# A graph network stack on one core: attention scores transposed once for four edge chunks, softmax results in four transposes, blocks 32 partitions apart

## The chip, the cores and the metric

The kernel runs on one core of a Trainium2 chip. The core's engines run side by side, each with its own queue of instructions in fixed order: TensorE (PE, matmuls and transposes through the array, with its weight loads listed as PEld), VectorE (DVE), ScalarE (ACT), GpSimd (POOL) and SyncE (SP, which issues DMAs). The metric is the device time of one execution in microseconds. Four timed runs of the kernel before took 3209.85 to 3216.49 us, with a median of 3212.87.

## The reference

The input is x, 128 graphs of 128 nodes with 256 features, and one 128 x 128 adjacency matrix. Four layers follow each other, each as layer_norm(x + layer(x)): a graph attention with four heads over 512 edges, a three-step convolution, a layer with three weight matrices and a bias, and a layer with two batch norms. The change touches only the first one, the attention:

```python
Xq = (H @ W_lin.T).reshape(bt, n, h, dh)
Xv = (H @ W_val.T).reshape(bt, n, h, dh)
e = jnp.einsum('behd,hd->beh', leaky_relu(Xq[:, src] + Xq[:, dst], 0.2), a)
e = e + jnp.log(A0[src, dst] + EPS)[None, :, None]
m = segment_max(e over edges with the same src)
ex = jnp.exp(e - m[src])
attn = ex / segment_sum(ex)[src]
Y = segment_sum(attn * Xv[:, dst])
return Y @ W_out.T
```

For each graph and head there is thus a score per edge, and a softmax over the edges that leave the same node.

## The kernel before

The 128 graphs are taken in 32 quads of 4 graphs. A quad has 4 graphs x 4 heads = 16 rows (R) of scores, and 512 edges (E), which lie sorted by their source node in 4 chunks (NE) of 128 edges.

The main loop, `iteration(k)` (lines 789 to 889), is a software pipeline: in one pass, quad k - 1 finishes its third layer and starts the fourth, quad k goes through the second layer's middle product (`second`, lines 520 to 606) and its last (`third`), quad k + 1 has its attention summed and starts the second layer, quad k + 2 (called e) has scores and softmax, and quad k + 3 (g) has its queries computed and its gathers issued. Passes k = 1 to 29 have a quad e. Quads 0, 1 and 2 have their scores and softmax in `start` and `iteration_0`. The order of the instructions on each engine is that of the code: the whole part stands under a manual schedule.

The steps of quad e that the change touches, in their order:

- `gather` and `gather_last` (POOL queue) bring the query rows of source and destination of each edge into a tile z of 128 edges x 1024; `score(k, c)` (lines 338 to 349) makes the leaky relu, the product with a and the sum over 64 features on DVE (L344, L346, L347). The 16 scores of 128 edges go to `es[:, c, :]`, edges on partitions. After the last chunk, L349 adds the logarithm of the weights.
- `softmax_parts(k)` (lines 351 to 371) is a generator whose pieces `iteration` calls between matmuls. Its first piece transposes the four chunks on PE (L356), each 128 x 16 to 16 x 128, side by side into one PSUM bank `pe`, so that 16 rows lie on partitions and 512 edges run along the row. The segment maximum is two running scans on DVE, forward (L358) and backward (L361), with a mask that resets them where the source node changes. L364 subtracts on DVE, L365 takes the exponent on ACT, and two more scans (L367, L369) make the segment sum.
- `attention(k)` (lines 373 to 383) turns exponent f and sum m back on PE in eight transposes of 16 x 128 to 128 x 16 (L379), takes the reciprocal (L381) and multiplies (L383) on DVE. `scatter` then writes the result to DRAM by four indirect DMAs from POOL's queue, and SP loads it as a dense matrix for the next pass.

In `iteration`, the first piece of the softmax is called after `stage_f` (L697, the fourth layer's first product of quad k - 1), and the others between the products of `queries` and `hidden` (L280 and L726), whose block sums are L180 to L190 on DVE. In `second`, `after(i)` calls what the list `between[i]` holds after the i-th product: scores of chunks 1 to 3 after products 0, 2 and 7, copies of attention rows after 1, 3, 8 and 10, and the transposes of the inputs of quad g (L237) after 11. After product 12 there is nothing in the list. `attention(e)` follows the first half of `third` (L616) and stands before `mix1` (L441).

PSUM has 8 banks, all handed out from one pool (`ps`).

Of the kernel before, what the change touches and what calls it, by code (L numbers as in the profile page):

```python
# [8 lines left out]
F32 = mybir.dt.float32  # L9
# [3 lines left out]
ALU = mybir.AluOpType  # L13
# [6 lines left out]
EPS = 1e-5  # L20
BIG = 1e38
DROP = -1e30


@with_exitstack
def gnn_stack(ctx: ExitStack, tc: tile.TileContext, x, adj, w_qv_t, a, w_out_t, src, dst,
# [14 lines left out]
    nc = tc.nc  # L41
    B, N, D = x.shape
    H, DH = a.shape
    E = src.shape[0]
    P = 128
    assert N == P and D == 2 * P and E == 4 * P and H * DH == D and DH == 64
    NE = E // P
# [3 lines left out]
    R = QB * H  # L51
# [9 lines left out]
    def ctile(shape, name, dtype=F32, pool=const):  # L61
        return pool.tile(shape, dtype, tag=name, name=name)

    def ps(name):
        return psum.tile([P, 512], F32, tag="ps", name=name)
# [6 lines left out]
    ident = ctile([P, P], "ident")  # L72
# [55 lines left out]
    with ExitStack() as phase:  # L128
        cst = phase.enter_context(tc.tile_pool(name="cst", bufs=1))
# [69 lines left out]
        ws = phase.enter_context(tc.tile_pool(name="ws", bufs=2))  # L199
        wk = phase.enter_context(tc.tile_pool(name="wk", bufs=2))  # L200
# [19 lines left out]
        keep_b = ctile([R, E], "keep_b", BF16, cst)  # L220
        reset_f = ctile([R, E], "reset_f", BF16, cst)
        reset_b = ctile([R, E], "reset_b", BF16, cst)


        def temp(name):
            return wk.tile([P, 512], F32, tag="t", name=name, bufs=6)

# [110 lines left out]
        def score(k, c):  # L338

            s = quads[k]  # L340
            if c == 0:
                s.es = ws.tile([P, NE, R], F32, tag="es", name=f"es{k}", bufs=1)
            z = s.z[c]
            nc.vector.scalar_tensor_tensor(z, z, SLOPE, z, op0=ALU.mult, op1=ALU.max)  # L344
            z3 = z.rearrange("p (b d) -> p b d", d=D)
            nc.vector.tensor_mul(z3, z3, a_bc.unsqueeze(1).to_broadcast([P, QB, D]))  # L346
            nc.vector.reduce_sum(s.es[:, c, :], z.rearrange("p (r d) -> p r d", d=DH), axis=AX.X)  # L347
            if c == NE - 1:
                nc.vector.tensor_add(s.es, s.es, log_col.unsqueeze(2).to_broadcast([P, NE, R]))  # L349

        def softmax_parts(k):

            s = quads[k]
            pe = ps("pe")
            for c in range(NE):
                nc.tensor.transpose(pe[:R, c * P:(c + 1) * P], s.es[:, c, :], ident)  # L356
            f = wk.tile([R, E], F32, tag="f", name="f", bufs=1)
            nc.vector.tensor_tensor_scan(f, reset_f, pe[:R, :], initial=0.0, op0=ALU.add, op1=ALU.max)  # L358
            yield
            m = wk.tile([R, E], F32, tag="m", name="m", bufs=1)  # L360
            nc.vector.tensor_tensor_scan(m[:, ::-1], reset_b[:, ::-1], f[:, ::-1], initial=0.0,  # L361
                                         op0=ALU.add, op1=ALU.max)
            yield
            nc.vector.tensor_sub(f, pe[:R, :], m)  # L364
            nc.scalar.activation(f, f, AF.Exp)  # L365
            yield
            nc.vector.tensor_tensor_scan(m, keep_f, f, initial=0.0, op0=ALU.mult, op1=ALU.add)  # L367
            yield
            nc.vector.tensor_tensor_scan(m[:, ::-1], keep_b[:, ::-1], m[:, ::-1], initial=0.0,  # L369
                                         op0=ALU.mult, op1=ALU.max)  # L370
            s.ex, s.den = f, m

        def attention(k):

            s = quads[k]
            pa = ps("pat")[:, :2 * NE * R].rearrange("p (s c r) -> p s c r", s=2, c=NE)
            for i, t in ((0, s.ex), (1, s.den)):
                for c in range(NE):
                    nc.tensor.transpose(pa[:, i, c, :], t[:, c * P:(c + 1) * P], ident[:R, :R])  # L379
            rden = wk.tile([P, NE, R], F32, tag="rden", name="rden", bufs=1)  # L380
            nc.vector.reciprocal(rden, pa[:, 1])  # L381
            s.at = wk.tile([P, NE, R], F32, tag="at", name="at", bufs=1)
            nc.vector.tensor_mul(s.at, rden, pa[:, 0])  # L383

        def scatter(k):
            s = quads[k]
# [64 lines left out]
        def first(k, i):  # L451
            s = quads[k]
            ph = ps("ph")
            for dc in range(DC):
                nc.tensor.matmul(ph, s.mx[i // 2 * 2][:, i % 2, dc, :], w1_sb[:, dc, :],
                                 start=(dc == 0), stop=(dc == DC - 1))
            h1 = temp("h1")
            nc.scalar.activation(h1, ph, AF.Relu)
            for c in range(K1):
                s.h1[i, c] = h1[:, c * P:(c + 1) * P]  # L460
# [328 lines left out]
        def iteration(k):  # L789
            a, c, b, e, g = k - 1, k, k + 1, k + 2, k + 3  # L790
            has_c, has_b, has_e, has_g = c < NQ, b < NQ, e < NQ, g < NQ
            if has_b and b > 2:
                quads[b].xr = load_x(b)
            if has_c:
                late_sums(c)
            parts = quads[a].layer2 if a > 0 else iter(())
            for _ in range(3):
                next(parts, None)
            if has_e:
                score(e, 0)  # L800
                gather_last(e)
            for _ in parts:
                pass
            if has_c:
                between = {i: [] for i in range(14)}
                if has_e:
                    for c_, i in enumerate((0, 2, 7)):
                        between[i].append(lambda c_=c_: score(e, c_ + 1))
                if has_b:
                    for j, i in enumerate((1, 3, 8, 10)):  # L810
                        between[i].append(lambda j=j: by_row(b, j))
                if has_g:
                    between[11].append(lambda: values_in(g, quads[g].xg))
                second(c, between)
            if has_g and g + 1 < NQ:
                quads[g + 1].xg = load_x(g + 1, "xg", 1, ws)
            if has_c:
                room = room_of("m2", 7)
            if has_g:
                q = queries(g, room[:5])  # L820
            stage_f(a)
            if not has_c:
                for i in range(K3):
                    hidden_last(a, i)
                return
            steps = softmax_parts(e) if has_e else iter(())
            next(steps, None)
            h = hidden(a, room[5:] + room[2:4])
            if has_g:
                run(q.p1, q.p5, q.p2)  # L830
                next(steps, None)
                q.p6()
            run(h.p1, h.p5)
            next(steps, None)
            if has_g:
                q.p7()
            run(h.p2, h.p6)
            next(steps, None)
            if has_g:
                run(q.p4, q.p3)  # L840
                spill(g)
            next(steps, None)
            h.p7()
            if has_b:
                aggregate(b)
            run(h.p4, h.p3)
            hidden_stats(a)
            if has_g:
                gather(g)
            if has_b:  # L850
                stage_a(b)
            next(steps, None)
            for _ in third(c, 0):
                pass
            if has_e:
                attention(e)
                scatter(e)
            rest = third(c, 2)
            if not has_b:
                next(rest)  # L860
                third_mix(c, 0)
                third_norm(c, 0)
                for _ in rest:
                    pass
                third_mix(c, 2)
                third_norm(c, 2)
                quads[c].layer2 = stage_e(c)
                next(quads[c].layer2)
                return
            mix1(b, 0)  # L870
            mix1(b, 2)
            third_mix(c, 0)
            next(rest)
            w = first_seven(b)
            third_norm(c, 0)
            next(rest)
            run(w.p1, w.p5, w.p2)
            next(rest)
            w.p6()
            next(rest, None)  # L880
            w.p7()
            third_mix(c, 2)
            w.p4()
            w.p3()
            third_norm(c, 2)
            quads[c].layer2 = stage_e(c)
            next(quads[c].layer2)
            for i in range(QB):
                mix2(b, i)

        def iteration_0():
# [14 lines left out]
            for _ in third(0, 0):  # L906
                pass
            steps = softmax_parts(2)
            next(steps)
            for j in (0, 1):  # L910
                by_row(1, j)
# [31 lines left out]
        def start():  # L943
# [106 lines left out]
                    nc.vector.tensor_copy(att_idx, pc[:, :, 0])  # L1050
                    nc.vector.tensor_copy(log_col, pc[:, :, 1])
            steps = softmax_parts(0)
            for _ in range(2):
                next(steps)
            values_in(2, quads[2].xr, nc.scalar.copy)
            next(steps)
# [65 lines left out]
            mix1(0, 2)  # L1122
            steps = softmax_parts(1)
            first(0, 0)
            next(steps)
            second_sums()
            for i in range(QB):
# [311 lines left out]
```

## Time and profile before

| | |
|---|---|
| median of four timed runs | 3212.87 us |
| the profiled execution, its own time | 3209.69 us |
| its span in the profile | 3208.0 us |
| PE busy, share of the span | 97% |
| DVE, ACT and POOL busy | 67%, 40% and 21% |
| score transposes on PE (L356) | 128, 273 ns each from start to modelled end |
| softmax transposes on PE (L379) | 256, 208 ns each |
| scans on DVE (L358, L361, L367, L369) | 32 of each, 1.20 to 1.21 us |
| reciprocal on DVE (L381) | 32, 556 to 558 ns |

A line of the profile in order of time has the start and the duration in microseconds, the engine, the line of the code, the operation with what it writes and reads, the shapes, and a count of merged instructions. For PE, 128*16 128x128 means a weight tile of 128 partitions x 16 columns and 128 x 128 moved values. Matmuls overlap in the array, so the distance between two starts says more than a duration. A bracket at the end of a line is the time that the engine was idle before, and what ended it.

### The profile page before, as it was taken

How to read it: one execution, taken by the hardware profiler on the slowest of the kernel's cores; microseconds unless marked ns; L12 is line 12 of the kernel's file. 1: busy time of each engine (PE TensorE's matmuls, PEld its weight loads, DVE VectorE, ACT ScalarE, POOL GpSimd, SP SyncE). 2: the span in 40 equal slices, each digit the busy share in tenths (PEclk: the TensorE clock that was granted, in tenths of full speed). 3: DMA queues.
4: the chain of work that ended last, by engine and by line, in shares of the span. 5: the costliest groups of instructions: out<-in, count | busy, mean ns of one | idle time of the engine just before them, and what ended most of it. 6: DMA issues, size and time to landing. Idle time of an engine off the chain costs nothing. (4 is left out here: it accounts for less than half of the span.)

```text
span 3208.0 us, 41204 instructions
## 1 busy us (share of the span) xinstructions
PE 3125.3 (97%) x15884; PEld 2589.4 (81%) x15884; DVE 2144.3 (67%) x4200; ACT 1277.8 (40%) x2229; POOL 662.7 (21%) x541
## 2 busy tenths in 40 slices
PE   6999999999999999999999999999999999999997
PEld 3788888888888888888888888888888888874444
DVE  6666666666666666666666666666666666437888
ACT  2343333333333343333333333343333333326668
POOL 4211222112111111222112111111222111001135
PEclk7999999999999999999999999999999999999999
DMA  7613333333333223333333333223333331005557
GB/s 217 182 50 96 106 99 106 98 94 106 101 91 104 88 77 96 106 99 106 99 93 106 100 92 104 87 76 97 106 99 106 99 87 53 21 27 184 177 194 272
DMA packets 118756, 344.86 MB, mean 108 GB/s; under 512 B 15008, under 2 KB 51744, under 8 KB 110240
## 3 DMA queue, kind: packets, MB, share of 16 engines
q0 software_dynamic: 45552, 151.55, 19.4%
q1 hardware_dynamic: 70960, 188.71, 16.3%
q8 instruction: 126, 2.06, 0.3%
q10 hardware_dynamic: 2048, 1.97, 0.2%
q14 instruction: 70, 0.57, 0.1%
HBM read 256.20 MB, written 85.98 MB: 107 GB/s over the span
## 5 line engine op out<-in xcount | busy, mean ns | idle before, releaser
L535 PE MATMUL ph<-m,w 128*128 128x256 f32 x2048 | 464.0, 380 | 0.0
L616 PE MATMUL p<-w,h 128*128 128x256 f32 x2048 | 462.3, 379 | 0.0
L616 PEld LDWEIGHTS p<-w,h 128*128 128x128 f32 x2048 | 389.0, 190 | 66.1 <-issue 7.7
L535 PEld LDWEIGHTS ph<-m,w 128*128 128x128 f32 x2048 | 387.4, 190 | 51.5
L329 POOL DMA_INDIRECT zs<-qd,src_idx x123 | 119.8, 974 | 1390.4 <-DVE z L739 706.0
L535 PE MATMUL ph<-m,w_s 128*128 128x256 f32 x1536 | 352.4, 379 | 0.0
L666 PE MATMUL po<-l2w,ms 128*128 128x256 f32 x1536 | 347.7, 379 | 1.3 <-DVE ms L658 1.3
L535 PEld LDWEIGHTS ph<-m,w_s 128*128 128x128 f32 x1536 | 291.8, 190 | 39.7
L666 PEld LDWEIGHTS po<-l2w,ms 128*128 128x128 f32 x1536 | 284.4, 190 | 36.2 <-DVE ms L658 1.5
L329 POOL DMA_INDIRECT zs<-qd,dst_idx x123 | 210.5, 1712 | 254.5 <-DMA zs<-qd,src_idx 243.3
L112 ACT ACTIVATE ln_sd<-ln_mv,eps 128x2 f32<-128x2 f32 x192 | 56.3, 293 | 496.7 <-DVE ln_mv L107 496.7
L548 DVE TENSOR_TENSOR h<-ph,u 128x512 f32<-128x512 f32 x128 | 88.1, 689 | 167.7 <-PE ph L535 114.5
L389 POOL DMA_INDIRECT attd<-at,att_idx x128 | 126.1, 985 | 351.3 <-DMA attd<-at,att_idx 248.0
L542 ACT COPY u<-ph 128x512 f32<-128x512 f32 x128 | 75.0, 586 | 244.2 <-PE ph L535 244.2
L346 DVE TENSOR_TENSOR zs<-zs,a_bc 128x1024 f32<-128x1024 f32 x123 | 150.8, 1226 | 4.2
L347 DVE TENSOR_REDUCE es<-zs 128x16 f32<-128x1024 f32 x123 | 150.1, 1220 | 4.2
L344 DVE SCALAR_TENSOR_TENSOR zs<-zs 128x1024 f32<-128x1024 f32 x123 | 149.6, 1217 | 2.1 <-DMA zs<-qd,dst_idx 2.1
L654 ACT COPY ms<-pm 128x512 f32<-128x512 f32 x128 | 71.2, 580 | 194.4 <-PE pm L652 191.0
L105 DVE BATCH_NORM_STATS2 ln_st<-xr 128x6 f32<-128x256 f32 x384 | 144.2, 417 | 5.5
L120 DVE TENSOR_SCALAR xr<-xr,ln_mv,ln_rs 128x256 f32<-128x256 f32 x384 | 143.1, 414 | 7.0
L477 DVE TENSOR_TENSOR h<-z,adc 128x512 f32<-128x512 f32 x62 | 41.9, 675 | 153.9 <-ACT adc L471 153.9
L640 POOL TENSOR_TENSOR xb<-xr,bias 128x512 f32<-128x512 f32 x64 | 81.6, 1275 | 298.3 <-DVE xr L120 160.3
(298 smaller groups left out, 5702.4 us busy)
## 6 DMA issues: line engine op xcount, KB each, us to landing
ad<-attd SPq DMA_DIRECT2D x32, 1024.0 KB, 4.8
zd<-z SPq DMA_DIRECT2D x31, 1024.0 KB, 7.4
zl<-zd SPq DMA_DIRECT2D x62, 512.0 KB, 3.5
xr<-in_x_dram SPq DMA_DIRECT2D x32, 512.0 KB, 5.8
x3d<-xr SPq DMA_DIRECT2D x32, 512.0 KB, 2.8
x3l<-x3d SPq DMA_DIRECT2D x32, 512.0 KB, 5.2
out_dram<-x3l POOLq DMA_DIRECT2D x31, 512.0 KB, 5.1
qd<-qt SPq DMA_DIRECT2D x30, 512.0 KB, 2.6
```

The lines of the kernel that those rows point to most:

```text
L105: nc.vector.bn_stats(st[:, i, :], r[:, i, :])
L120: nc.vector.tensor_scalar(r[:, i, :], r[:, i, :], mv[:, i, 0:1], rs[:, i:i + 1], op0=ALU.subtract, op1=ALU.mult)
L329: nc.gpsimd.indirect_dma_start(out=s.z[c], out_offset=None, in_=s.qd, in_offset=bass.IndirectOffsetOnAxis(ap=idx[:, c:c + 1], axis=0), com ...
L344: nc.vector.scalar_tensor_tensor(z, z, SLOPE, z, op0=ALU.mult, op1=ALU.max)
L346: nc.vector.tensor_mul(z3, z3, a_bc.unsqueeze(1).to_broadcast([P, QB, D]))
L347: nc.vector.reduce_sum(s.es[:, c, :], z.rearrange("p (r d) -> p r d", d=DH), axis=AX.X)
L389: nc.gpsimd.indirect_dma_start(out=ad, out_offset=bass.IndirectOffsetOnAxis(ap=att_idx[:, c:c + 1], axis=0), in_=s.at[:, c, :], in_offset= ...
L535: nc.tensor.matmul(bank[g][:, i].rearrange("p b n -> p (b n)"), wa[:, c, f:f + P], s.m2[:, blk_b, c].rearrange("p b n -> p (b n)"), start= ...
L548: nc.vector.tensor_add(block(g, row, col), bank[g], kept_[g])
L616: nc.tensor.matmul(p3[:, t * D:(t + 1) * D], s.h2[f // 2][:, f % 2, j + t, :], w3_sb[:, f, :], start=(f == 0), stop=(f == K2 - 1))
L640: nc.gpsimd.tensor_add(s.xb[:, j:j + 2, :], xj, bias.unsqueeze(1).to_broadcast([P, 2, D]))
L666: nc.tensor.matmul(po[:, i % 2, :], mss[i][:, t, dc, :], l2w[:, t, dc, :], start=(n3 == 0), stop=(n3 == 3 * DC - 1))
```

## The change

Two tiles are made once and cleared: `scores`, 128 edges x 4 chunks x 32 places, of which the first 16 hold scores, and `pair`, 48 partitions x 512 edges. A constant GAP = 32 is the distance of blocks.

The scores of all four chunks are transposed as one 128 x 128 matrix: chunk c comes out on partitions 32 c to 32 c + 15. Four copies on ACT put the four blocks side by side into partitions 0 to 15 of `pair` (f). The scans and the subtract read f in SBUF where they read PSUM before. The last scan writes the sum to partitions 32 to 47 of `pair`. So exponent and sum of a chunk lie in one tile of 48 partitions, and `attention` turns them back with one transpose a chunk: columns 0 to 15 are the exponent, 32 to 47 the sum.

The generator has one piece more, since transpose and copies are now apart from the first scan. In `iteration` that new first piece is called in `second` after product 12, and the piece with the first scan stays after `stage_f`, as do all later ones. In `start` and `iteration_0` there is one more call at the old place of the first.

```diff
+        scores = ctile([P, NE, GAP], "scores", pool=cst)
+        pair = ctile([GAP + R, E], "pair", pool=cst)
+        nc.vector.memset(scores, 0.0)
+        nc.vector.memset(pair, 0.0)
...
-                s.es = ws.tile([P, NE, R], F32, tag="es", name=f"es{k}", bufs=1)
+                s.es = scores[:, :, :R]
...
-            pe = ps("pe")
+            f, m = pair[:R], wk.tile([R, E], F32, tag="m", name="m", bufs=1)
+            rows = f
+            pe = ps("pe")[:, :P]
+            nc.tensor.transpose(pe, scores.rearrange("p c r -> p (c r)"), ident)
             for c in range(NE):
-                nc.tensor.transpose(pe[:R, c * P:(c + 1) * P], s.es[:, c, :], ident)
-            f = wk.tile([R, E], F32, tag="f", name="f", bufs=1)
-            nc.vector.tensor_tensor_scan(f, reset_f, pe[:R, :], initial=0.0, op0=ALU.add, op1=ALU.max)
+                nc.scalar.copy(f[:, c * P:(c + 1) * P], pe[c * GAP:c * GAP + R, :])
             yield
-            m = wk.tile([R, E], F32, tag="m", name="m", bufs=1)
-            nc.vector.tensor_tensor_scan(m[:, ::-1], reset_b[:, ::-1], f[:, ::-1], initial=0.0,
+            nc.vector.tensor_tensor_scan(m, reset_f, rows, initial=0.0, op0=ALU.add, op1=ALU.max)
+            yield
+            nc.vector.tensor_tensor_scan(m[:, ::-1], reset_b[:, ::-1], m[:, ::-1], initial=0.0,
                                          op0=ALU.add, op1=ALU.max)
             yield
-            nc.vector.tensor_sub(f, pe[:R, :], m)
+            nc.vector.tensor_sub(f, rows, m)
...
-            nc.vector.tensor_tensor_scan(m[:, ::-1], keep_b[:, ::-1], m[:, ::-1], initial=0.0,
+            nc.vector.tensor_tensor_scan(pair[GAP:, ::-1], keep_b[:, ::-1], m[:, ::-1], initial=0.0,
                                          op0=ALU.mult, op1=ALU.max)
-            s.ex, s.den = f, m
...
-            pa = ps("pat")[:, :2 * NE * R].rearrange("p (s c r) -> p s c r", s=2, c=NE)
-            for i, t in ((0, s.ex), (1, s.den)):
-                for c in range(NE):
-                    nc.tensor.transpose(pa[:, i, c, :], t[:, c * P:(c + 1) * P], ident[:R, :R])
+            pa = ps("pat")[:, :NE * (GAP + R)].rearrange("p (c r) -> p c r", c=NE)
+            for c in range(NE):
+                nc.tensor.transpose(pa[:, c, :], pair[:, c * P:(c + 1) * P], ident[:GAP + R, :GAP + R])
...
-            nc.vector.reciprocal(rden, pa[:, 1])
+            nc.vector.reciprocal(rden, pa[:, :, GAP:])
...
-            nc.vector.tensor_mul(s.at, rden, pa[:, 0])
+            nc.vector.tensor_mul(s.at, rden, pa[:, :, :R])
...
+            steps = softmax_parts(e) if has_e else iter(())
             if has_c:
                 between = {i: [] for i in range(14)}
+                between[12].append(lambda: next(steps, None))
...
-            steps = softmax_parts(e) if has_e else iter(())
             next(steps, None)
```

More of the change, by code (lines that the diff above doesn't have):

```diff
@@ L22 @@
 DROP = -1e30
+GAP = 32
 @with_exitstack
@@ L908, in iteration_0 @@
             steps = softmax_parts(2)
+            next(steps)
             next(steps)
@@ L1052, in start @@
             steps = softmax_parts(0)
-            for _ in range(2):
+            for _ in range(3):
                 next(steps)
@@ L1124, in start @@
             first(0, 0)
+            next(steps)
             next(steps)
```

## The prediction

> **What bounds the kernel now.** I read the page's busy table first, then a table by stage for one pass of the main loop, then the instructions in order of time: TensorE (PE) alone, and ScalarE (ACT) and VectorE (DVE) around the places that the change touches. The chain that ended last holds only the last microsecond, so it does not help.
>
> The busy table, and one pass (here 1425.50 to 1512.70 us: total, then busy time of PE, PE weight load, DVE, ACT and POOL, granted clock, DMA share, GB/s):
>
> ```profile
> PE 3125.3 (97%) x15884; PEld 2589.4 (81%) x15884; DVE 2144.3 (67%) x4200; ACT 1277.8 (40%) x2229; POOL 662.7 (21%) x541
> ...
> 1425.50:1512.70 87.20, 87.20 (x469) 76.10 (x468) 58.40 (x113) 32.92 (x56) 17.02 (x14) 1.00 0.34 98
> ```
>
> PE is busy for all 87.20 us of the pass, at full clock; DVE and ACT have 28.8 and 54.3 us to spare. So in a steady pass only PE time counts, as long as no wait is made. Next, PE in order of time (start, duration, engine, line, tiles, count):
>
> ```profile
> 1443.50 1.04 PE L237 MATMUL pt<-ident,xg 128*128 128x128 f32 x8
> 1444.37 1.89 PE L535 MATMUL ph<-m,w 128*128 128x256 f32 x8
> 1446.10 1.89 PE L535 MATMUL ph<-m,w_s 128*128 128x256 f32 x8
> 1447.83 1.95 PE L697 MATMUL pa<-ahat_t,xr 128*128 128x128 f32 x16
> 1449.61 0.60 PE L356 MATMUL pe<-ident,es 128*16 128x128 f32 x4
> 1450.05 1.03 PE L280 MATMUL y<-wqv,xt 128*128 128x256 f32 x4
> ...
> 1474.68 0.41 PE L379 MATMUL pat<-ident,f 16*128 16x16 f32 x4
> 1474.95 0.39 PE L379 MATMUL pat<-ident,m 16*128 16x16 f32 x4
> 1475.28 2.05 PE L441 MATMUL pm<-wt_t,xr 128*128 128x128 f32 x16
> ```
>
> Matmuls overlap, so I price by the distance from start to start. The four score transposes hold PE for 1450.05 - 1449.61 = 0.44 us (0.11 each). Eight whole 128x128 transposes (L237) take 1444.37 - 1443.50 = 0.87, also 0.109 each: a transpose's price here follows its 128 moved columns, not the 16 or 128 weight columns. The eight softmax transposes take 1475.28 - 1474.68 = 0.60: 0.27 for the first four (0.0675 each), 0.33 for the last four with the change back to full matmuls. Last, the covers on DVE and ACT (a bracket is idle time and what ended it):
>
> ```profile
> 1441.78 0.23 DVE L349 TENSOR_TENSOR es<-es,log_col 128x64 f32<-128x64 f32 x1
> 1446.79 0.62 ACT L552 ACTIVATE h<-h 128x512 f32<-128x512 f32 x1
> 1448.75 0.63 ACT L552 ACTIVATE h<-h 128x512 f32<-128x512 f32 x1 [1.34 <-DVE h L548]
> 1449.42 1.31 ACT L700 COPY ag<-pa 128x512 f32<-128x512 f32 x2
> 1450.25 1.21 DVE L358 TENSOR_TENSOR_SCAN f<-reset_f,pe 16x512 f32<-16x512 bf16 x1
> ```
>
> **The change part by part.** Passes k = 1 to 29 have a softmax: 29 steady ones. Quads 0, 1 and 2 have theirs in the start.
>
> *Scores.* Four transposes become one of the same form as L237: 0.44 - 0.11 = 0.33 saved on PE, 29 x 0.33 = 9.6 us. Bounds 0.27 (one semaphore event, 0.05 in the rows of L356, lands on PE) to 0.35.
>
> The Trainium skill, "TensorE: Matmul & The Clock Gate", section "LDWEIGHTS (loading the stationary operand)", speaks against this: it prices a weight load at columns / 1.2 ns, so 128 columns cost an estimated 107 ns where 16 cost 13, and if that stood in the open the saving would fall by 29 x 0.09 = 2.7 us; L237's 0.109 with the same load says it is hidden.
>
> *Place.* The transpose moves from behind L697 to before the last product of the second layer: start 1446.10 instead of 1449.61. It waits for L349, which ends at 1442.01: 4.1 us of slack (at k = 1, where L349 starts at 219.30 and that product at 221.29, 1.8). Behind it in PE's queue stand that product, L697 and everything after. They come 0.11 later until L697 ends and 0.33 earlier from L280 on. No DMA issue moves on any queue, POOL's and SP's order is the old one.
>
> *Four ACT copies* replace nothing. Bounds: the 128x256 copy (L503) takes 0.37, the 128x512 one 0.59 (L542), so 0.84 ns per column and about 0.27 for 128 columns; back to back, two 512-column copies of L654 take 1.05, 0.11 less than twice 0.58. So four take 0.27 + 3 x 0.16 = 0.75 at best and 4 x 0.37 = 1.49 at worst; I take 0.85, between single and overlapped copies of their own size. They stand between the two relus above, where ACT is idle for 1.34 us: nothing. At 1.49 they push the second relu and the L700 copies by 0.15; those end at 1450.73 and PE first reads them at 1453.50. Cover gone by 2.6 us more would be needed before PE noticed. The first scan, at 1450.25, waits for these copies (about 1448.3) instead of PE: nothing.
>
> *DVE.* Scans and subtract stay in their places with the same sizes (1.20 and 0.68); reading f from SBUF instead of PSUM is bounded by L358's 1.208 against L361's 1.203. DVE runs on 0.11 late while PE runs 0.33 early, so DVE loses 0.44 of lead: the block sum of L188 ends at 1452.11 and PE wants it at 1454.37; the exponent's input is ready at 1455.46 and ACT, with its table load, asks at 1456.46. Both leads outlive 0.44. The two clears go to DVE before its first input lands (it idles 5.4 us until 7.06): nothing.
>
> *PSUM.* One bank is asked for earlier and given back after the copies instead of after the subtract (1455.46). In the built order L697's second bank now follows a relu that ended at 1442.57; PE wants it at about 1448. No wait.
>
> *Softmax transposes.* Eight become four, with 48 rows and 48 moved columns instead of 16. Each is at least the 0.0675 of today and at most the 0.109 of a full one. 0.0675 at 16 columns and 0.109 at 128 are the nearest rows; I take 0.095, because the weight load is seen not to be pulled ahead here (0.33 us idle on PEld before L379), and then the 32 extra columns come on top at the 0.85 ns of L237 (0.027). So 4 x 0.095 + 0.06 for the change back = 0.44, which saves 0.16; 29 x 0.16 = 4.6 us. With the bounds 0.10 to 0.27: 2.9 to 7.8.
>
> The Trainium skill, "TensorEngine Tiling (Array Packing)", section "Key Properties", says that a change of tiling mode drains TensorE. At L379 the trace shows it (0.09 us before, and it stays, since 48 rows are a part of the array too); at L356 it shows none: L697's sixteen take 1.78 = 16 x 0.111 into it. By the rule the score part would save another drain at each end, an estimated 29 x 0.18 = 5 us; by the rows nothing, and I take the rows.
>
> *Once.* The start is not PE-bound:
>
> ```profile
> 97.50 0.60 PE L356 MATMUL pe<-ident,es 128*16 128x128 f32 x4
> 97.76 0.60 ACT L458 ACTIVATE h<-ph 128x512 f32<-128x512 f32 x1 [1.24 <-PE ph L455]
> 98.14 1.21 DVE L358 TENSOR_TENSOR_SCAN f<-reset_f,pe 16x512 f32<-16x512 bf16 x1 [2.78 <-PE pe L356]
> 106.93 0.63 ACT L365 ACTIVATE f<-f 16x512 f32<-16x512 f32 x1 [2.56 <-DVE f L364]
> 108.08 2.08 PE L498 MATMUL pm<-wt_t,h 128*128 128x128 f32 x8 [2.15 <-ACT h L458]
> ...
> 2675.91 1.10 PE L726 MATMUL z<-ag,l3w_s 128*128 128x256 f32 x4 [1.06 <-DVE ag L188]
> ```
>
> Quad 1: the copies queue behind L458 (to 98.3), so the scan starts near 99.25; DVE has no gap until the subtract, the exponent is 1.1 late, the relu behind it too, and PE at 108.08: +1.1. Quad 0: copies 0.85 - 0.5 from the faster transposes (slower clock there), about +0.3 on a chain to the attention load. Quad 2: -0.3. At k = 29 the scan no longer waits for PE in front of the block sums, and the 1.06 wait of the last row goes: -1.0. Together +0.1, bounds -1.5 to +1.5.
>
> **Sum.** -9.6 - 4.6 + 0.1 = -14.1 against the profiled execution's own 3209.69 us (span 3208.0): 3195.6. That execution lies 3.2 below the median of the four timed runs, 3212.87; on the median's scale 3198.8. I forecast 3199.
>
> **Rivals.**
> - *Only the scores pay.* If four 48-row transposes take what eight took (0.135 each, the duration of today's 16*128 weight load), 29 x 0.33 = 9.6 is left: 3203. For it: that load is not overlapped with the matmul before it. Against: two of today's, load and all, fit in 0.135.
> - *Hidden anyway.* If something beside PE set the pass at 87.2, nothing moves: 3210 to 3213. Against: no PE wait in a steady pass, 54 us of idle ACT, a third of the DMA.
> - *Slower: PE waits for the scores at the new place.* One mechanism: the last chunk's gather lands late, L349 follows, and PE, in order, stands still before the last product. At k = 1 DVE does wait 2.15 us for that gather and the slack is down to 1.8. It decides when the scores come 4.6 us later than in the pass shown (4.1 of slack and the 0.49 won); each further microsecond costs 29. A wait of 1 us a pass makes 3199 + 29 = 3228. Against: DVE's scores run without a DMA wait in the pass shown, and all that feeds them moves with PE.
> - *The change isn't made.* Excluded: the built program has 1 and 4 transposes a quad, and four copies.
>
> **How the numbers follow.** As forecast 0.72; only scores 0.13; hidden 0.06; slower by a new wait 0.09. About 0.2% (6.4 us) is what a measurement of this kernel can tell from no change. Likeliest case alone: gains of 29 x 0.37 - 1.5 = 9.2 to 29 x 0.62 + 1.5 = 19.5, that is 3193 to 3204, and 1 us for the scatter of the medians: 3192 to 3205. The range over all, 3191 to 3206, takes in the second case. Faster 0.84 (both gaining cases less a little), same 0.07, slower 0.09.
>
> **What would show it.** Right: a steady pass of 86.6 to 86.8 us, still all PE; one pe transpose holding PE 0.11; four pat transposes from 0.33 to 0.50 to the next matmul; ACT's four copies between the relus; no wait of PE on L349's successor. Wrong: PE idle before the pe transpose or before the hidden products, copies over 0.4 us each, or pat transposes over 0.13 each.

## The result and the profile after

The changed kernel takes 3217.25 us (median of 32 runs, 3215.42 to 3218.97), the kernel before 3213.49 (52 runs, 3208.55 to 3216.91). The ratio is 1.0015, with a 95% interval of 1.001 to 1.002: slower by 0.15%, within the 0.2% that was called no change. The forecast was 3199, range 3191 to 3206. The profiled execution of the changed kernel has a span of 3215.4 us, the one of before 3208.0.

First the busy table of the kernel after:

```profile
PE 3119.5 (97%) x15660; PEld 2574.0 (80%) x15660; DVE 2147.9 (67%) x4202; ACT 1302.3 (41%) x2357; POOL 663.5 (21%) x541
```

PE has 224 instructions fewer, ACT 128 more. The change is made as described, and yet PE is not done earlier. A steady pass runs from the first fourth-layer product (called pa here, after the tile that it writes) to the same product one pass later. Before, it took 87.47 us, from 1447.83, shown in the prediction, to 1535.29 (with unrounded starts). PE in order of time, before:

```profile
1456.95 1.03 PE L726 MATMUL y<-ag,l3w_s 128*128 128x256 f32 x4
1457.82 1.03 PE L280 MATMUL y<-wqv_s,xt 128*128 128x256 f32 x4
1458.68 1.03 PE L280 MATMUL z<-wqv,m 128*128 128x256 f32 x4
...
1535.29 1.95 PE L697 MATMUL pa<-ahat_t,xr 128*128 128x128 f32 x16
```

and after:

```profile
1453.94 0.27 PE L365 MATMUL pe<-ident,scores 128*128 128x128 f32 x1
1454.05 1.89 PE L543 MATMUL ph<-m,w_s 128*128 128x256 f32 x8
1455.78 1.95 PE L705 MATMUL pa<-ahat_t,xr 128*128 128x128 f32 x16
1457.56 1.03 PE L288 MATMUL y<-wqv,xt 128*128 128x256 f32 x4
...
1464.47 1.03 PE L734 MATMUL y<-ag,l3w_s 128*128 128x256 f32 x4
1465.78 1.13 PE L288 MATMUL y<-wqv_s,xt 128*128 128x256 f32 x4 [0.28 <-ACT m L305]
1466.75 1.03 PE L288 MATMUL z<-wqv,m 128*128 128x256 f32 x4
1467.61 1.03 PE L734 MATMUL y<-m,l3w_s 128*128 128x256 f32 x4
...
1482.75 0.44 PE L387 MATMUL pat<-ident,pair 48*128 48x48 f32 x4
1483.12 2.05 PE L449 MATMUL pm<-wt_t,xr 128*128 128x128 f32 x16
...
1543.25 1.95 PE L705 MATMUL pa<-ahat_t,xr 128*128 128x128 f32 x16
```

The pass is 1543.25 - 1455.78 = 87.47 us, as before. Read from start to start, the scores' transpose holds PE 0.11 us (1453.94 to 1454.05) where four held 0.44: 0.33 won. The four softmax transposes hold it 0.37 (1482.75 to 1483.12) where eight held 0.60: 0.23 won, and 0.22 by the lengths of whole passes below. And one line has a bracket that the kernel before did not have: `y<-wqv_s,xt` waits for a copy on ACT. Its predecessor takes 1465.78 - 1464.47 = 1.31 us from start to start instead of 0.86, and it takes 0.97 itself instead of 0.86: 0.45 and 0.11, together 0.55 us lost with unrounded starts. PE makes this wait 28 times in the kernel, 7.9 us of idle time together. What was won in two places is lost in a third. Why the copy is late is seen in ACT's order, shown with the subtract on DVE, in the kernel before:

```profile
1454.57 0.59 ACT L730 COPY m<-y 128x512 f32<-128x512 f32 x1 [0.28 <-PE y L726]
1454.78 0.68 DVE L364 TENSOR_TENSOR f<-pe,m 16x512 f32<-16x512 f32 x1
1455.17 1.28 ACT L365 ACT_TABLE_LOAD   x1
1456.46 0.63 ACT L365 ACTIVATE f<-f 16x512 f32<-16x512 f32 x1
1457.00 0.56 ACT L297 COPY m<-y 128x512 f32<-128x512 f32 x1
```

and in the kernel after:

```profile
1455.15 1.05 ACT L367 COPY pair<-pe 16x128 f32<-16x128 f32 x4
1456.71 0.63 ACT L560 ACTIVATE h<-h 128x512 f32<-128x512 f32 x1 [0.51 <-DVE h L556]
...
1462.08 0.58 ACT L738 COPY m<-y 128x512 f32<-128x512 f32 x1 [0.28 <-PE y L734]
1462.58 0.68 DVE L374 TENSOR_TENSOR pair<-pair,m 16x512 f32<-16x512 f32 x1
1463.34 1.28 ACT L375 ACT_TABLE_LOAD   x1 [0.67 <-DVE pair L374]
1464.63 0.63 ACT L375 ACTIVATE pair<-pair 16x512 f32<-16x512 f32 x1
1465.17 0.56 ACT L305 COPY m<-y 128x512 f32<-128x512 f32 x1
```

Before, the 1.28 us in which ACT loads the exponent's table start as soon as the copy in front is done (1455.17), beside the subtract on DVE, which ends at 1455.46. After, ACT stands idle for 0.67 us until the subtract is done (1463.26), and only then loads the table. The copy that PE wants is queued behind the exponent and ends at 1465.73. PE would have been ready for it at 1464.47 + 0.86 = 1465.33.

The order of the built program on ACT tells where the wait sits (LoadActFuncSet is the table load, EventSemaphore an instruction that holds a wait and nothing else; a semaphore named after an engine is raised by that engine):

```
before  L365 LoadActFuncSet
        L365 Activation f<-f 16x512 [waits DVE_49]
after   L375 EventSemaphore [waits DVE_49]
        L375 LoadActFuncSet
        L375 Activation pair<-pair 16x512 [waits Activation_49]
```

Before, the exponent waits for one thing, DVE's subtract, and the load ahead of it waits for nothing. After, the tile `pair` was also written by ACT's own four copies, so the exponent waits for two things, and one of the two waits has moved ahead of the load, into an instruction of its own. It is the one for the subtract, the later of the two. This is the order at 31 of the 32 exponents of the changed kernel.

### The profile page after: what moved, and what is told of

It reads as the page before. It is cut to its first block, busy times and chain, and to the rows that moved or that the text cites. A ratio compares the mean times of both kernels' runs of the same rounds, so it can differ in the third digit from the quotient of the medians.

```text
span 3215.4 us, 40942 instructions
## 1 busy us (share of the span) xinstructions
PE 3119.5 (97%) x15660; PEld 2574.0 (80%) x15660; DVE 2147.9 (67%) x4202; ACT 1302.3 (41%) x2357; POOL 663.5 (21%) x541
## 5 line engine op out<-in xcount | busy, mean ns | idle before, releaser
L355 DVE TENSOR_REDUCE scores<-zs 128x16 f32<-128x1024 f32 x123 | 150.0, 1220 | 4.2
```

## The experiments

Theory T: this load behind the wait costs 0.55 us a pass, and that it equals the 0.55 won is chance. Rival R: the pass is held at 87.47 by something else, whatever PE saves. Rival C: the four copies themselves make ACT late.

### The table loaded early

In the changed kernel, one more exponent, of one column, stands in `softmax_parts` ahead of the second scan:

```diff
+        warm = ctile([P, 1], "warm", pool=cst)
...
             yield
+            nc.scalar.activation(warm, eps, AF.Exp)
             nc.vector.tensor_tensor_scan(m[:, ::-1], reset_b[:, ::-1], m[:, ::-1], initial=0.0,
```

> The changed kernel with one more exponent, of one column, issued on ScalarE ahead of the second scan's subtract, so that the exponent's table is loaded while ScalarE is idle and not behind the wait for the subtract. Theory T (the table load that has come to stand behind that wait costs PE 0.55 us a pass at the product y<-wqv_s,xt): a steady pass of 86.92 us (87.47 less 0.55), the wait of PE on m at that product gone, 28 passes x 0.55 = 15 us less, and 2 to 7 us less in the start, where the load of 109.59 also stands behind the wait: 3195 to 3200. Rival R (something beside PE sets the pass at 87.47, whatever PE saves): 87.47 and about 3217. Rival C (the four copies on ScalarE are what makes the product late): the wait stays, a pass of 87.3 to 87.5, 3212 to 3217.

3198.29 us (3197.07 to 3199.44), ratio to the kernel before 0.9951 [0.9937, 0.9964]. ACT in this kernel:

```profile
1446.46 1.28 ACT L372 ACT_TABLE_LOAD   x1
1447.76 0.20 ACT L372 ACTIVATE warm<-eps 128x1 f32<-128x1 f32 x1
1448.45 0.58 ACT L306 COPY m<-y 128x512 f32<-128x512 f32 x1 [0.49 <-PE y L289]
1449.31 0.58 ACT L740 COPY m<-y 128x512 f32<-128x512 f32 x1 [0.28 <-PE y L736]
1450.59 0.63 ACT L377 ACTIVATE pair<-pair 16x512 f32<-16x512 f32 x1 [0.69 <-DVE pair L376]
```

and PE:

```profile
1443.01 1.95 PE L707 MATMUL pa<-ahat_t,xr 128*128 128x128 f32 x16
...
1451.70 1.03 PE L736 MATMUL y<-ag,l3w_s 128*128 128x256 f32 x4
1452.56 1.03 PE L289 MATMUL y<-wqv_s,xt 128*128 128x256 f32 x4
...
1529.93 1.95 PE L707 MATMUL pa<-ahat_t,xr 128*128 128x128 f32 x16
```

The exponent still waits for the subtract, but the load is over by then. The bracket on PE is gone, and the pass is 1529.93 - 1443.01 = 86.92 us: the full 0.55 won. R and C fall: nothing else holds the pass at 87.47, and the copies are still on ACT.

### Each half alone

The softmax half, in the kernel before:

```diff
+        pair = ctile([32 + R, E], "pair", pool=cst)
+        nc.vector.memset(pair, 0.0)
...
-            f = wk.tile([R, E], F32, tag="f", name="f", bufs=1)
+            f = pair[:R]
...
-            nc.vector.tensor_tensor_scan(m[:, ::-1], keep_b[:, ::-1], m[:, ::-1], initial=0.0,
+            nc.vector.tensor_tensor_scan(pair[32:, ::-1], keep_b[:, ::-1], m[:, ::-1], initial=0.0,
...
+            for c in range(NE):
+                nc.tensor.transpose(pa[:, c, :], pair[:, c * P:(c + 1) * P], ident[:32 + R, :32 + R])
```

> The kernel before with the softmax half of the change alone: exponents and sums in one tile 32 partitions apart, four transposes of 48 rows instead of eight; scores as before, the exponent waits for the subtract alone. T: the saving of 0.22 us a pass that the trace of the changed kernel shows at these transposes comes through: a pass of 87.25, about 29 x 0.22 = 6 us less, 3207. R: 87.47 and 3213. C: as T, since the copies are not there.

3205.86 us (3202.89 to 3206.94), ratio 0.9972 [0.9961, 0.9983]; the pass is 87.25 us. The exponent writes the same shared tile here, but no ACT copy has written it, and the load keeps its place ahead of the wait.

The scores half, in the changed kernel (one transpose and four copies stay, the softmax goes back to two tiles and eight transposes):

```diff
-            f, m = pair[:R], wk.tile([R, E], F32, tag="m", name="m", bufs=1)
+            f, m = (wk.tile([R, E], F32, tag=t, name=t, bufs=1) for t in "fm")
...
+            for i, t in ((0, s.ex), (1, s.den)):
+                for c in range(NE):
+                    nc.tensor.transpose(pa[:, i, c, :], t[:, c * P:(c + 1) * P], ident[:R, :R])
```

> The changed kernel with the scores half alone: one transpose for the scores and four copies, but eight transposes for the softmax from two tiles as before. The exponent still waits for both the subtract and ScalarE's own copies. T: 0.33 won at the transposes and 0.55 lost at the product behind the exponent, a pass of 87.69, about 3222 to 3225. R: 87.47 and about 3217. C: as T.

3229.04 us (3223.48 to 3230.21), ratio 1.0042 [1.0028, 1.0055], somewhat above what was expected; the pass, expected at 87.69, is 87.70:

```profile
1461.82 1.95 PE L705 MATMUL pa<-ahat_t,xr 128*128 128x128 f32 x16
...
1549.52 1.95 PE L705 MATMUL pa<-ahat_t,xr 128*128 128x128 f32 x16
```

So alone the scores half loses 0.22 us a pass net (0.33 won, 0.55 lost), and the softmax half wins 0.22. The sum is the zero of the whole change, and it is chance. The 3229 lies 4 to 7 us above T's number, though one of the five runs, 3223.48, meets it. The profiled execution, one of the long ones, has the excess at both ends. The first pa stands at 234.09 us, at 231.12 in the changed kernel and at 223.01 in the one before. From the last pa to the end it takes 332.7 us, the changed kernel 328.9, with a granted clock of 0.87 against 0.96 in the first 40 us of that stretch.

### The late load by itself

In the kernel before, without any part of the change, one copy of a column onto itself takes the wait for the subtract and stands ahead of the load:

```diff
+            nc.scalar.copy(f[:, :1], f[:, :1])
             nc.scalar.activation(f, f, AF.Exp)
```

> The kernel before with one added instruction: ScalarE copies one column of f onto itself ahead of the exponent, so that this copy takes the wait for the subtract and the table load stands behind it. No transpose and no copy of the change. T: the load starts after the subtract, the exponent about 1.2 us later than now; 0.9 of that is not covered before PE asks for m, less what PE is later here than in the changed kernel (0.33 to 0.44): a pass of 87.8 to 88.0, 3223 to 3229. R: 87.47 and 3213. C: 87.47 and 3213.

3225.19 us (3223.74 to 3226.25), ratio 1.0034 [1.0022, 1.0046]; the pass is 87.90. ACT:

```profile
1466.27 0.19 ACT L365 COPY f<-f 16x1 f32<-16x1 f32 x1 [0.34 <-DVE f L364]
1466.47 1.28 ACT L366 ACT_TABLE_LOAD   x1
1467.77 0.63 ACT L366 ACTIVATE f<-f 16x512 f32<-16x512 f32 x1
1468.31 0.56 ACT L297 COPY m<-y 128x512 f32<-128x512 f32 x1
```

and PE:

```profile
1467.73 1.03 PE L727 MATMUL y<-ag,l3w_s 128*128 128x256 f32 x4
1468.91 1.13 PE L280 MATMUL y<-wqv_s,xt 128*128 128x256 f32 x4 [0.16 <-ACT m L297]
1469.88 1.03 PE L280 MATMUL z<-wqv,m 128*128 128x256 f32 x4
```

The same wait appears at the same product, and costs 1.18 - 0.86 = 0.32 there and 0.97 - 0.86 = 0.11 behind it: 0.43 a pass. The added copy is not what makes the exponent late: it is over 7.87 us after pa (1466.47 - 1458.60), and before, the exponent started at 8.63. A load behind the wait is enough for the loss.

### The copies on VectorE

```diff
-                nc.scalar.copy(f[:, c * P:(c + 1) * P], pe[c * GAP:c * GAP + R, :])
+                nc.vector.tensor_copy(f[:, c * P:(c + 1) * P], pe[c * GAP:c * GAP + R, :])
```

> The changed kernel with the four copies on VectorE in place of ScalarE. The exponent then depends on VectorE alone, so its table load has no second wait to stand behind. T: the load runs ahead again and the loss goes without any added instruction: a pass of 86.92, or up to 87.1, since the copies (about 0.7 us in VectorE's order) make the exponent's input later and use up what is left of its lead; with the start 3197 to 3204. C, in the form that is left after the one-column exponent removed the loss with the copies in place (that it was the added exponent's own doing, and the wait for ScalarE's copies still matters): also 86.9. Should the load stay behind the subtract: 87.5 to 88.0 and 3217 or more.

3195.59 us (3194.43 to 3197.12), ratio 0.9945 [0.9931, 0.9959]: the lowest median here, though the interval overlaps that of the early table. The pass is 1530.30 - 1443.38 = 86.92 us. Nothing was added; the exponent merely has one source again, and in the built program the load has no wait and stands where it stood before. PE and ACT:

```profile
1443.38 1.95 PE L705 MATMUL pa<-ahat_t,xr 128*128 128x128 f32 x16
...
1449.68 0.59 ACT L738 COPY m<-y 128x512 f32<-128x512 f32 x1 [0.28 <-PE y L734]
1450.29 1.28 ACT L375 ACT_TABLE_LOAD   x1
1451.58 0.63 ACT L375 ACTIVATE pair<-pair 16x512 f32<-16x512 f32 x1
1452.12 0.56 ACT L305 COPY m<-y 128x512 f32<-128x512 f32 x1
...
1530.30 1.95 PE L705 MATMUL pa<-ahat_t,xr 128*128 128x128 f32 x16
```

The four copies take 1.18 us on DVE (ACT: 1.05). They start after 0.82 us of idle DVE and make nothing late: the subtract ends at 1450.86, in the middle of the load.

### Control: the early table in the kernel before

The line of the first experiment, in the kernel before.

> The kernel before with the same one-column exponent ahead of the subtract, as a control. T: the table load there never stood behind the wait and the exponent had its lead, so nothing is won in a pass: 87.47, and within 0.1% of the kernel before; in the start quad 0's load, which follows two copies there, may run earlier by up to 0.7 us. If the one-column exponent gained by itself, by whatever way: a pass under 87.3.

3212.22 us (3208.36 to 3216.45), ratio 1.0 [0.9991, 1.0009], pass 87.47. The one-column exponent gains nothing of its own; it gains only where the load stood behind the wait. Its start shows how far a first pa moves without any of the change: the profiled execution is 0.8 us ahead of the one before at the attention's output in the start (L432, 156.97 against 157.76), and 2.7 behind at the first pa (225.74 against 223.01). In the sixteen matmuls of L432 its granted clock was 0.68, against 1.00 before.

### The start without copies

The changed kernel with the early table from quad 3 on; quads 0 to 2 have four transposes again, and their first scan reads PSUM:

```diff
+            if k < 3:
+                pe = ps("pe")
+                rows = pe[:R, :]
+                for c in range(NE):
+                    nc.tensor.transpose(pe[:R, c * P:(c + 1) * P], scores[:, c, :R], ident)
...
+            if k > 2:
+                nc.scalar.activation(warm, eps, AF.Exp)
```

> The changed kernel with the one-column exponent from quad 3 on, and with quads 0, 1 and 2, whose softmax stands in the start, scored as in the kernel before: four transposes, the scan straight from PSUM, no copies. If the copies are what still costs in the start (pa of k = 1 at 226.1 us against 223.0): a pass of 86.92 and 3194 to 3197. If the start's remaining 3 us are due to the clock's phase alone: 3197 to 3200.

3198.96 us (3196.66 to 3199.69), ratio 0.9954 [0.9941, 0.9968]: no better than with the copies in the start, so the first of the two expectations was missed. In the profiled executions this kernel is 3.3 us ahead of the first experiment's at the products of L669 in the start (160.92 against 164.19), and 1.5 ahead at the first pa (224.61 against 226.08). It was 4.8 ahead where the attention's output starts (L447, 154.32 against 159.15); the same sixteen matmuls then took 6.76 us at a granted clock of 0.54, in the first experiment 5.21 at 0.71. Between 180 and 200 us its granted clock was 0.91, the other's 1.00. Why the clock differs there no run shows, and one profile of each does not settle what the copies in the start cost.

## Why the prediction was wrong

**Scores, 0.33 a pass: right.** It is what is left between the softmax half alone and the whole change with the load out of the way: 87.25 - 86.92 = 0.33. The further 0.18 a pass that the prediction worked out from a rule on tiling, and set aside, is not seen.

**Softmax transposes, 0.16 a pass: right in kind, too small.** 0.22 by the softmax half alone (87.47 - 87.25), within the bounds of 0.10 to 0.27. The term that was too big is the price of a transpose, 0.095. The four take 0.37 with the change back, not 0.44, and start 0.06 apart behind the first (1482.85, 1482.91, 1482.97), as the eight of before do: the 32 additional rows and columns show no cost.

**ACT copies, hidden: right.** 1.05 us instead of 0.85, and 0.51 us of idle ACT are left behind them. As work they cost nothing. What they cost came by another way.

**DVE: this is the step that failed.** It read "the exponent's input is ready at 1455.46 and ACT, with its table load, asks at 1456.46. Both leads outlive 0.44". The lead of one microsecond existed only as long as the load could run ahead of the exponent's wait. That was taken from the trace of before as if it belonged to the exponent, and it belonged to the form of its wait. The four copies gave the exponent a second thing to wait for, the load went behind the wait for the subtract, and the 1.28 us came to stand in series. Measured from pa, the exponent starts 8.85 us in (1464.63 - 1455.78), where it started at 8.63 before and starts at 8.20 with the copies on DVE (1451.58 - 1443.38), while PE wants the copy behind it 0.44 us earlier than before. The spare time of 0.26 us that this copy had (it ended at 1457.56, PE's product started at 1457.82) does not cover 0.22 + 0.44. The price of the step is 0.55 us a pass, 28 x 0.55 = 15.4 us of the 19.0 between the medians of the changed kernel and the first experiment. Their two profiled executions are 20.1 us apart, 5.0 of them ahead of the first pa (231.12 and 226.08) and 15.1 behind it. It could have been read without a chip: the order of the built program shows the wait ahead of the load.

The Trainium skill, "Perfetto Trace Analysis", section "Identifying Dependency Chains", says that "instructions waiting on multiple engines may have EventSemaphore instructions inserted prior to the instruction with additional wait conditions". The EventSemaphore of the changed kernel is such a case, and the 0.67 us bracket on the load adds to the sentence that the table load comes after what is inserted.

**Once, +0.1: wrong at both ends.** At k = 29 the pass lost 0.97 us (82.91 to 81.94). The forecast was 1.0 for the wait alone, on top of what every pass was to gain. Of the 0.97, 0.44 and 0.22 are the transposes (the one for the scores stands ahead of pa now), so only about 0.3 is left for the wait. PE's idle 1.06 did not go; two shorter waits took its place, the first for ACT's copies of pa, which the block sums on DVE now wait for, too:

```profile
2682.05 1.13 PE L734 MATMUL y<-ag,l3w 128*128 128x256 f32 x4 [0.28 <-ACT ag L708]
2683.43 1.10 PE L734 MATMUL z<-ag,l3w_s 128*128 128x256 f32 x4 [0.24 <-DVE ag L189]
```

In the start the profiled execution of the changed kernel is 8.1 us behind at the first pa (231.12 against 223.01). Of these, 3.4 are there where the attention's output starts (161.17 against 157.76), 2.8 come in its sixteen matmuls, whose granted clock was 0.56 against 1.00, and 1.9 behind them. How much of the 4.7 from there on is due to the change is not shown: the control loses 3.5 between the same two places. Quad 1 is where the load shows again:

```profile
109.59 1.28 ACT L375 ACT_TABLE_LOAD   x1 [5.43 <-DVE pair L374]
110.88 0.63 ACT L375 ACTIVATE pair<-pair 16x512 f32<-16x512 f32 x1
...
112.04 1.87 PE L506 MATMUL pm<-wt_t,h 128*128 128x128 f32 x8 [5.02 <-ACT h L466]
```

PE's wait of 2.15 us before L498 became one of 5.02. With the table loaded early and the copies still on ACT the same wait is 3.74: 1.6 for the copies, forecast 1.1, and 1.3 for the load.

**The pass itself.** The forecast looked for "86.6 to 86.8 us" in place of 87.20. The window of 87.20 was not quite a full pass; a pass is 87.47, and the forecast gain of 0.49 would have made it 86.98. With the load out of the way it is 86.92.

**The rivals.** "Hidden anyway" (3210 to 3213) came nearest in time, and its reason is refuted: PE does set the pass. "Slower" named a wait at the scores' new place, and no wait is seen there. None of the rivals named a wait for ACT. The sum of the gains came out near without the load: -14.1 us was forecast, and the changed kernel with the load moved out of the way stands at 0.9951 of before, about -15.7. Part of that closeness is luck, since a pass wins 0.55 instead of 0.49 and the two ends do worse than forecast.

## What to carry to other kernels

When a change gives an ACT function a second producer (here ACT's own copies into the tile that the exponent reads), look in the built program where the table load ahead of it stands: it may have come behind a wait, and then its 1.28 us are no longer hidden. Keep one producer for such an operand, or trigger the load earlier by a one-column call of the same function in a gap of ACT. And a lead read from a trace holds for the waits of that program only; where a change alters what an instruction waits for, the lead has to be worked out anew.

## What the runs showed of the hardware

- The table load took 1.28 us in every row. The Trainium skill, "ScalarE: Activation LUTs", section "What ACT_TABLE_LOAD costs", gives about 1283 ns, and adds a drain of about 1380 ns for a switch. No such drain is seen here: with the table loaded early, the load starts at 1446.46, 0.02 us after a copy's end, and the next activation 0.02 us after the load's end.
- A wait of PE costs more than its idle time. The bracket said 0.28 us, the loss was 0.55: 0.45 until the product started and 0.11 more until the next one did. The bracket counts from the modelled end of the product before (1464.47 + 1.03), while products that don't wait start 0.86 apart. With the late load by itself it was 0.16 in the bracket and 0.43 in the pass.
- Transposes of 48 x 128 and of 16 x 128 tiles start the same 0.06 us apart. With the first one's start and the change back to full matmuls included, four of the former hold PE 0.37 us and eight of the latter 0.59 to 0.60.
- In the start the granted clock differs between executions with nearly the same waits. The sixteen matmuls of the attention's output stand behind a wait of 3.9 to 4.0 us for ACT in each of these profiles. They took 3.72 us at a granted clock of 1.00 before, 5.41 at 0.68 in the control, 6.23 at 0.59 with the softmax half alone, 6.54 at 0.56 after and 6.76 at 0.54 in the last experiment. That is 3.7 us divided by the clock. What sets the clock there no run shows. Before:

```profile
157.76 3.72 PE L430 MATMUL po<-wo,yt 128*128 128x256 f32 x16 [3.91 <-ACT yt L419]
```

After:

```profile
161.17 6.54 PE L438 MATMUL po<-wo,yt 128*128 128x256 f32 x16 [3.88 <-ACT yt L427]
```
